# Two more quarter products by seven products, and x's two slots laid apart

## The chip, the cores and the metric

One core of a Trainium2 chip runs the whole kernel in one launch. The metric is the device time of that launch in microseconds (us), the median of several runs. A profile of one execution gives, for each instruction, its engine, its start and its length, all counted from the start of the profiled span. Five engines work side by side: TensorE (PE, matrix products; PEld is its loading of weights), VectorE (DVE), ScalarE (ACT), GpSimd (POOL) and SyncE (SP), which here only issues transfers. Transfers run on 16 DMA engines that all queues share.

## The reference

Four graph layers over the same 2048 x 2048 adjacency matrix `adj` and a batch `x` of 8 x 2048 nodes x 64 features, all fp32. Each layer adds its result to x and normalizes over the features.

```python
# layer 0: Chebyshev sum with weights that depend on the node
As = [eye, A, 2.0 * (A @ A) - eye]
w = einsum('nd,dkio->nkio', embedding, weight)      # d = 16
b = einsum('nd,do->no', embedding, bias)
x_g = einsum('knm,bmc->bnkc', stack(As), x)
x = layernorm(x + einsum('bnki,nkio->bno', x_g, w) + b)
# layer 1: twice relu((A @ z) @ W_i)
x = layernorm(x + z)
# layer 2: x @ w_self + (A @ x) @ w_neighbor + bias
x = layernorm(x + ...)
# layer 3: [x, Ax, 2AAx - x, Ax, 2AAx - x] @ weight + bias   (both supports are adj)
x = layernorm(x + ...)
```

So adj is applied to a 2048 x 512 matrix again and again. The first of these products, `A x` of layer 0, is the place of this change.

## The kernel before

**Layout.** The 2048 nodes are cut into 16 tiles of 128 (`NT`); the batch gives 512 columns (`BF`), handled as four pairs (`NP`) of two batch items x 64 features = 128 columns. `xy` holds x for every node tile and, in a second slot, another 512 columns per tile that serve as scratch and later as a second activation. In the kernel before, the two slots of a tile lie side by side in a partition: `[P, NT, 2, BF]`.

**Matrix products by seven.** A product of two 2 x 2 block matrices needs eight block products; with sums of blocks formed beforehand, seven do. The kernel uses this twice, one level inside the other. Seven big products stand for the whole of adj (`A11`, `A12`, `A22` and the sums `S1` to `S4`), and each of these may again be made of seven small ones with sums of its own quarter (`inner` in `prepare`, which writes four such sums; the function `inner` in `product` uses them). The sums of adj are formed once, in the first product, written to `comb` in DRAM, and read back by all later products (`load`, `product`).

**The first product, slice by slice.** adj comes in four slices of 512 output nodes (every slice takes one node tile out of each group of four), and each slice in four chunks `a` of 1 MB (`slice_chunk`), chunk j holding the inputs of node tiles 4j to 4j+3. `slices` are read into four ring buffers. While TensorE multiplies a slice, VectorE forms its sums (`prepare`, a generator that is advanced by `next(parts)` at chosen places), and GpSimd issues their stores to `comb`.

- Slice 0 (`plain_slice`) can't use sums of x yet, since x is still coming in. Chunks 2 and 3 (`AHEAD = (2, 3, 0, 1)`) are multiplied plainly for all four batch pairs, 32 matmuls of 512 columns into four PSUM banks (L868): for the first chunk node tile by node tile, for the second pair by pair. Chunks 0 and 1, that is the quarters (I, J) = (0, 0) and (1, 0) of adj, go through `two_level`: 28 matmuls of 128 columns (L828) that stand for 32, ScalarE copying each of the seven results out of PSUM (L832), and VectorE joining them (L843, L846) and adding the plain part (L887). Its sums of x, `t1`, lie in the scratch slot of `xy`.
- Slices 1 to 3 (`fast_slice`) use the seven big products with sums of x (`T`), matmuls of 256 columns (L914). One of them, with A22, goes through `two_level`.
- Between the products the pump (`pump.step`) puts small TensorE jobs: the biases (L735) and the turning back of each slice's result `hT` to node order (`back`, L461).

**What sets the order.** Instructions marked `keep_in_program_order` stay in the order of the program on their engine; the rest is placed by a scheduler. VectorE's sums are all marked. A transfer counts its completion on one of eight semaphores used in turn, for SyncE and ScalarE together, and waits until the transfer eight places before it is done. A buffer of a ring is written again when its last reader is through: `C` (four buffers, the `inner` sums), `T` (three, the big sums), `t` (five, the results `hT`), `a` (four, the chunks).

**The loads at the start.** SyncE issues the first chunk in four pieces of one node tile (L158), ScalarE x of the same four tiles in four pieces (L168: 128 columns of the first tile, its other 384, the second tile, the last two together). Then SyncE issues in turn x and a of the chunks 3, 0 and 1 (L171, L158). Before data is there, 11 matmuls on zeros keep TensorE busy (`rise`, L720).

Of the kernel before, what the change touches and what calls it, by code (L numbers as in the profile page):

```python
# [16 lines left out]
P = 128  # L17
EPS = 1e-5
GW = 512
# [85 lines left out]
def kernel(  # L105
# [42 lines left out]
    xy = big.tile([P, NT, 2, BF], F32, tag="xy", name="xy")  # L148
# [4 lines left out]
    def slice_chunk(ns, j, parts=1):  # L153

        a = ring.tile([P, TG, NG, P], F32, tag="a", name="a")
        for c in range(parts):
            m = ts(c, TG // parts)
            nc.sync.dma_start(a[:, m], slices[ns, j][:, m])  # L158
        return a
# [4 lines left out]
    chunks[0, AHEAD[0]] = slice_chunk(0, AHEAD[0], TG)  # L164

    for t, n, cols in ((0, 1, slice(0, 2 * F)), (0, 1, slice(2 * F, BF)), (1, 1, slice(0, BF)), (2, 2, slice(0, BF))):
        t += AHEAD[0] * TG
        nc.scalar.dma_start(xy[:, t : t + n, 0, cols], x[:, t : t + n, cols])  # L168
    for j in AHEAD[1:]:
        tq = slice(j * TG, (j + 1) * TG)  # L170
        nc.sync.dma_start(xy[:, tq, 0, :], x[:, tq, :])  # L171
        chunks[0, j] = slice_chunk(0, j)
# [12 lines left out]
    def xcol(slot, t, p):  # L185
        return xy[:, t, slot, ts(p, 2 * F)]

    def part(g, p, slot):
        return xy[:, g * TG : (g + 1) * TG, slot, ts(p, 2 * F)]
# [25 lines left out]
    def product(src, feature, between=None, rate=1, own=None, pin=False, runs=None, onto_slot=None, ends=False):  # L215
# [6 lines left out]
        def quarter(h, c):  # L222

            return xy[:, h * NT // 2 : (h + 1) * NT // 2, src, c * 4 * F : (c + 1) * 4 * F]
# [232 lines left out]
    def to_nodes(dst, pool, tiles, p, hT):  # L457
# [4 lines left out]
        nc.scalar.copy(xy[:, tiles, dst, ts(p, 2 * F)], pt)  # L462
# [4 lines left out]
    class Norm:  # L467
# [9 lines left out]
        def flat(self):  # L477
            return xy[:, self.tiles, self.slot, self.p0 * 2 * F : (self.p0 + self.n) * 2 * F]
# [59 lines left out]
        def store(self, t0=0, t1=TG):  # L538
            tiles = slice(self.tiles.start + t0, self.tiles.start + t1)
            for k in range(self.n):  # L540
                p = self.p0 + k
                nc.sync.dma_start(out[:, p, tiles], xy[:, tiles, self.slot, ts(p, 2 * F)])
# [38 lines left out]
    if True:  # L581
# [48 lines left out]
        def prepare(ns, ch, outers):  # L630
# [48 lines left out]

            outers[A22] = inner(A22, *raw(1, 1))  # L680
            yield
            inner(A12, *raw(0, 1))
            if ns == 0:

                sums_of_blocks()
                outers[A11] = inner(A11, *raw(0, 0))
                outers[A21] = inner(None, *raw(1, 0))
            outers[S1] = s1 = outer(rq(1, 0), rq(1, 1), ALU.add)
# [9 lines left out]
            if ns:  # L698
# [11 lines left out]
        with tc.tile_pool(name="p_n", bufs=4, space=PSUM) as p_n, tc.tile_pool(  # L710
# [30 lines left out]
            def xq(h, c):  # L741

                v = xy[:, h * NT // 2 : (h + 1) * NT // 2, 0, c * 4 * F : (c + 1) * 4 * F]
# [6 lines left out]
                xy[:, 3:NT:TG, 1, :].rearrange("p t (h c) -> p t h c", h=2),  # L750
                xy[:, 2:NT:TG, 1, :].rearrange("p t (h c) -> p t h c", h=2),
# [40 lines left out]
            def sums_t(b, t):  # L792
# [7 lines left out]
            b1 = [  # L800
                [by_tiles(xy[:, j * TG : (j + 1) * TG, 0, ts(2 * c + p, 2 * F)]) for j in range(2) for p in range(2)]
                for c in range(2)
            ]
            t1 = [[by_tiles(xy[:, c:NT:TG, 1, ts(n, 2 * F)]) for n in range(4)] for c in range(2)]
# [5 lines left out]
            def sums_of_blocks():  # L810
                for c in range(2):
                    sums_t(b1[c], t1[c])

            def two_level(raw, sums_, b, t, out):
# [11 lines left out]
                def mul(ps, n, x, start, to):  # L826
# [9 lines left out]
                mul(pa, 1, b21, False, out[:, 0, 0])  # L836
                mul(pb_, 6, t3, False, part[:, 2])
                mul(pa, 4, t1, True, out[:, 1, 1])
                mul(pb_, 3, t4, False, out[:, 0, 1])
                mul(pa, 7, b22, False, out[:, 1, 0])  # L840
                o = out.rearrange("p a b n -> p (a b) n")
                pin = tc.keep_in_program_order
                pin(nc.vector.tensor_tensor(  # L843
                    o[:, 1:], o[:, 1:], part[:, 0].unsqueeze(1).to_broadcast([P, 3, P]), ALU.add
                ))
                pin(nc.vector.tensor_tensor(o[:, 2:], o[:, 2:], part[:, 1:], ALU.add))  # L846
# [4 lines left out]
            def by_blocks(v):  # L851
                return v.rearrange("p (a b n) -> p a b n", a=2, b=2)
# [5 lines left out]
            def plain_slice(ns, ch, outers):  # L858


                ps = [bank() for p in range(NP)]
# [384 lines left out]
```

## Time and profile before

| | us |
|---|---|
| median of 3 runs | 1667.22 |
| all runs | 1666.92 to 1667.96 |
| profiled execution, its own time | 1667.24 |
| its span, first to last instruction | 1665.5 |

The first 200 us, and the end, in stretches: busy time of each engine and, in brackets, its instructions; then the granted clock of TensorE (1.00 is full), the share of time the DMA engines were busy, and what they moved.

| stretch, us | what runs | PE busy | DVE busy | PEclk | DMA share | GB/s |
|---|---|---|---|---|---|---|
| 0 to 6 | warming matmuls | 4.94 | 0.17 | 1.00 | 0.59 | 160 |
| 6 to 34 | slice 0, chunks 2 and 3 | 28.00 | 15.53 | 1.00 | 0.99 | 370 |
| 34 to 59 | slice 0, four quarters | 25.00 | 24.80 | 1.00 | 0.87 | 318 |
| 59 to 111 | slice 1 | 51.58 | 48.16 | 1.00 | 0.99 | 365 |
| 111 to 200 | slices 2 and 3 | 89.00 | 66.42 | 1.00 | 0.88 | 317 |
| 1640 to 1666 | the end | 18.39 | 18.03 | 0.92 | 0.25 | 73 |

How to read the profile: a line of the timeline gives the start, the busy time, the engine, the source line, the operation, the tile written and the tiles read, their shapes and the count; in brackets stands the idle time before it and what ended that. An fp32 matmul leaves two records, so x64 are 32 matmuls. Records of matmuls overlap, so the time of one is read from the distance between starts. L12 is line 12 of the kernel. In a row on a load, the last number is the time from its issue to its landing.

### The profile page before, as it was taken

Reading aid. Unit: us, or ns where it says so; the run is one execution under the profiler, and the core shown is the slowest. Engines: PE = TensorE matmul, PEld = TensorE weight load, DVE = VectorE, ACT = ScalarE, POOL = GpSimd, SP = SyncE. Lnnn points to the kernel's source line nnn. Section 1 sums busy time; section 2 is a strip of 40 time slices with the busy share of each in tenths; the row PEclk is TensorE's granted clock in tenths of the full one; section 3 lists DMA queues with packets and bytes.
Section 4 is the critical chain, followed back from the end, with each engine's and each line's share of the span. In section 5 each row is a group of like instructions: output and inputs, shape, how many; then the busy total and the mean of one; then the engine's idle time right before and its main releaser. Section 6 shows DMA issues by size and latency. Waiting matters only on the chain.

```text
span 1665.5 us, 21273 instructions
## 1 busy us (share of the span) xinstructions
PE 1656.5 (99%) x8414; PEld 1060.5 (64%) x8414; DVE 965.7 (58%) x1737; ACT 276.2 (17%) x811; POOL 245.6 (15%) x332
## 2 busy tenths in 40 slices
PE   9999999999999999999999999999999999999998
PEld 6988844444444444444454455599998455579998
DVE  5986895656456456655434365873668344453657
ACT  0200110242142144430010011220001011100001
POOL 1221200254155056550000000000000000000000
PEclk9999999999999999999999999999999999999999
DMA  8998899504503600029878877667888856678894
GB/s 316 339 385 310 319 319 326 201 26 163 204 26 128 250 26 26 26 67 363 291 262 279 303 256 258 231 213 275 292 295 300 304 210 237 227 263 297 311 317 162
DMA packets 82499, 391.57 MB, mean 235 GB/s; under 512 B 8960, under 2 KB 25600, under 8 KB 42848
## 3 DMA queue, kind: packets, MB, share of 16 engines
q1 hardware_dynamic: 69584, 346.78, 59.2%
q0 software_dynamic: 11248, 42.08, 6.7%
q10 hardware_dynamic: 1568, 1.35, 0.3%
q8 instruction: 67, 1.10, 0.3%
q14 instruction: 32, 0.26, 0.0%
HBM read 339.85 MB, written 50.33 MB: 234 GB/s over the span
## 4 chain that ended last, share of the span: by engine, by line
PE 99%; DVE 0%; ACT 0%; issue 0%; DVEq 0%; ACTq 0%
PE y L1089 20%; PE mmb L276 17%; PE mma L276 12%; PE mmc L276 12%; PE mmb L269 9%; PE ps_n L914 7%; PE mma L269 6%; PE mmc L269 6%; PE ps_i L828 3%; PE z L1141 3%; PE z L1170 2%; PE ps_n L868 2%; PE pt L1132 1%; PE pt_n L461 0%; PE rise L720 0%; PE mmd L269 0%
## 5 line engine op out<-in xcount | busy, mean ns | idle before, releaser
L276 PE MATMUL mmb<-a,t 128*128 128x512 f32 x648 | 292.0, 593 | 0.0
L1099 DVE SCALAR_TENSOR_TENSOR xy<-y,e_sb,xy 128x128 f32<-128x128 f32 x512 | 179.6, 351 | 141.2 <-PE y L1089 125.3
L276 PEld LDWEIGHTS mmb<-a,t 128*128 128x128 f32 x648 | 121.5, 190 | 145.3 <-issue 143.3
L1108 POOL TENSOR_TENSOR s<-s 128x512 f32<-128x512 f32 (+2 forms) x192 | 157.1, 818 | 333.4 <-ACT s L1103 323.2
L1103 ACT ACTIVATE s<-y,e_sb 128x128 f32<-128x128 f32 x512 | 139.2, 383 | 231.6 <-PE y L1089 231.6
L227 DVE TENSOR_TENSOR u<-mmb,p 128x512 f32<-128x512 f32 x84 | 57.9, 689 | 177.6 <-PE mmb L276 122.2
L269 PE MATMUL mmb<-t,a 128*128 128x128 f32 x1344 | 156.9, 275 | 0.0
L269 PEld LDWEIGHTS mmb<-t,a 128*128 128x128 f32 x1344 | 153.4, 192 | 0.0
L1089 PE MATMUL y<-wn,xT 64*128 64x512 f32 x512 | 131.5, 590 | 0.0
L1089 PE MATMUL y<-wn,C 64*128 64x512 f32 x512 | 131.2, 589 | 0.0
L1089 PE MATMUL y<-wn,tT 64*128 64x512 f32 x512 | 131.2, 589 | 0.0
L276 PE MATMUL mma<-a,T 128*128 128x512 f32 x256 | 115.5, 594 | 0.0
L276 PE MATMUL mmc<-a,t 128*128 128x512 f32 x216 | 97.3, 592 | 0.0
L291 ACT COPY p<-mma 128x512 f32<-128x512 f32 x42 | 24.7, 588 | 404.6 <-PE mma L276 247.3
L1089 PEld LDWEIGHTS y<-wn,xT 64*128 64x128 f32 x512 | 49.3, 187 | 61.2 <-issue 60.7
L1089 PEld LDWEIGHTS y<-wn,C 64*128 64x128 f32 x512 | 49.6, 187 | 60.2 <-issue 60.2
L1089 PEld LDWEIGHTS y<-wn,tT 64*128 64x128 f32 x512 | 49.6, 187 | 60.3 <-issue 60.3
L276 PE MATMUL mma<-a,xy 128*128 128x512 f32 x192 | 86.7, 593 | 0.0
L276 PEld LDWEIGHTS mma<-a,T 128*128 128x128 f32 x256 | 47.6, 190 | 56.8 <-issue 56.5
L227 DVE TENSOR_TENSOR C<-mmc,C 128x512 f32<-128x512 f32 x48 | 33.2, 692 | 85.9 <-PE mmc L276 75.1
L276 PEld LDWEIGHTS mmc<-a,t 128*128 128x128 f32 x216 | 40.0, 190 | 45.4 <-issue 45.2
L1141 PEld LDWEIGHTS z<-wd,C 128*128 128x128 f32 x384 | 50.2, 191 | 21.8 <-issue 20.8
(157 smaller groups left out, 2113.3 us busy)
## 6 DMA issues: line engine op xcount, KB each, us to landing
a<-comb SPq DMA_DIRECT2D x240, 1024.0 KB, 4.8
a<-in_blocks SPq DMA_DIRECT2D x54, 1024.0 KB, 4.8
comb<-si POOLq DMA_DIRECT2D x28, 1024.0 KB, 6.3
a<-in_slices SPq DMA_DIRECT2D x15, 1024.0 KB, 9.0
comb<-so POOLq DMA_DIRECT2D x15, 512.0 KB, 8.5
t1T<-hT SPq DMA_DIRECT2D x16, 256.0 KB, 3.9
xT<-in_xT SPq DMA_DIRECT2D x16, 256.0 KB, 3.3
tT<-t1T SPq DMA_DIRECT2D x16, 256.0 KB, 3.2
```

Source lines behind the costliest of these rows:

```text
L227: nc.vector.tensor_tensor(out, a, b, op)
L269: nc.tensor.matmul(to, a[:, k, m, :], xb[:, m, :], start=(start and opens and m == 0), stop=(m == TG - 1), skip_group_check=True,)
L276: nc.tensor.matmul(ps, xb[:, m, :], a[:, :, m, :], start=(start and m == 0), stop=(m == TG - 1), skip_group_check=True,)
L828: nc.tensor.matmul(ps, x[:, m // 2, m % 2], s[n](m), start=(start and m == 0), stop=(m == TG - 1), skip_group_check=True,)
L868: mm = nc.tensor.matmul(ps[p], xcol(0, TG * j + m, p), ch[j][:, m], start=(n == 0 and m == 0), stop=(n == 1 and m == TG - 1), skip_group_c ...
L914: nc.tensor.matmul(ps[:, ts(p, GW // 2)], b(k, p), a(k // TG, k % TG), start=(start and p == k == 0), stop=(k == NT // 2 - 1), skip_group_ ...
L1089: mm = nc.tensor.matmul(y[:, b, :], terms[n][half, ts(k, P)], wn[half, n, h * DH : (h + 1) * DH, :], start=(n == 0), stop=(n == 2),)
L1099: nc.vector.scalar_tensor_tensor(acc, y[:, :, ts(d, F)], e, acc, ALU.mult, ALU.add)
L1103: nc.scalar.activation(s[:, d], y[:, :, ts(d, F)], AF.Copy, scale=e)
L1108: nc.gpsimd.tensor_tensor(s[:, :n], s[:, :n], s[:, n : 2 * n], ALU.add)
L1141: nc.tensor.matmul(z[:, k, :], aT[:, ts(k, P)], wd[:, w, :], start=(n == 0), stop=(n == len(terms) - 1),)
L1170: nc.tensor.matmul(z[n][:, k], xT[half, ts(k, P)], w[half], start=True, stop=True)
```

## The change

Five things are done at once.

1. Slice 0: of the plain product of chunks 2 and 3, the part for the output half I = 1 and the batch pairs 2 and 3 (the quarter J = 1, c = 1) goes through `two_level`, with A22's sums and four new sums of x. The plain matmuls of pairs 2 and 3 then have 256 columns and share one PSUM bank. Their order is new: for both chunks, first pairs 0 and 1 node tile by node tile, then pairs 2 and 3.
2. Slice 1: the product of A11, sixteen plain matmuls of 256 columns, goes through `two_level` with the sums of x that slice 0 used. A11's sums are therefore formed ahead of A12's.
3. `two_level` becomes a generator that yields between its matmuls and its closing adds, and these are three (of 256, 256 and 128 columns) instead of two (384 and 256).
4. `xy` becomes `[P, 2, NT, BF]`: a slot's 16 tiles are contiguous in a partition. All accesses to it follow.
5. The first chunk is loaded in three pieces, of one, one and two node tiles.

```diff
-    xy = big.tile([P, NT, 2, BF], F32, tag="xy", name="xy")
+    xy = big.tile([P, 2, NT, BF], F32, tag="xy", name="xy")
...
-    chunks[0, AHEAD[0]] = slice_chunk(0, AHEAD[0], TG)
+    chunks[0, AHEAD[0]] = slice_chunk(0, AHEAD[0], (1, 1, 2))
...
-        nc.sync.dma_start(xy[:, tq, 0, :], x[:, tq, :])
+        nc.sync.dma_start(xy[:, 0, tq, :], x[:, tq, :])
...
+            if ns == 0:
+                sums_of_blocks((1, 1))
             outers[A22] = inner(A22, *raw(1, 1))
             yield
+            if ns == 1:
+                outers[A11] = inner(A11, *raw(0, 0))
             inner(A12, *raw(0, 1))
             if ns == 0:
-                sums_of_blocks()
+                sums_of_blocks((0, 0), (0, 1))
+                yield
+            if ns == 0:
                 outers[A11] = inner(A11, *raw(0, 0))
                 outers[A21] = inner(None, *raw(1, 0))
+                yield
...
-            if ns:
+            if ns >= 2:
                 inner(A11, *raw(0, 0))
...
-                mul(pa, 7, b22, False, out[:, 1, 0])
-                o = out.rearrange("p a b n -> p (a b) n")
-                pin = tc.keep_in_program_order
-                pin(nc.vector.tensor_tensor(
-                    o[:, 1:], o[:, 1:], part[:, 0].unsqueeze(1).to_broadcast([P, 3, P]), ALU.add
-                ))
-                pin(nc.vector.tensor_tensor(o[:, 2:], o[:, 2:], part[:, 1:], ALU.add))
+                mul(pa, 7, b22, False, out[1][:, 0])
+                yield
+                def add(a, b):
+                    tc.keep_in_program_order(nc.vector.tensor_tensor(a, a, b, ALU.add))
+                add(part[:, 1:], part[:, :1].to_broadcast([P, 2, P]))
+                add(out[1], part[:, 1:])
+                add(out[0][:, 1], part[:, 0])
+                yield
...
-                ps = [bank() for p in range(NP)]
+                ps = [bank() for p in range(3)]
                 for n, j in enumerate(AHEAD[:2]):
-                    steps = [(p, m) for p in range(NP) for m in range(TG)]
-                    if n == 0:
-                        steps = [(p, m) for m in range(TG) for p in range(NP)]
-                    for k, (p, m) in enumerate(steps):
+                    for p, m in [(p, m) for m in range(TG) for p in range(2)] + [(p, m) for p in (2, 3) for m in range(TG)]:
+                        to, cols = ps[p] if p < 2 else ps[2][:, ts(p - 2, GW // 2)], NG if p < 2 else NG // 2
                         mm = nc.tensor.matmul(
-                            ps[p],
+                            to,
                             xcol(0, TG * j + m, p),
-                            ch[j][:, m],
+                            ch[j][:, m, :cols],
...
                 hT = [new_h() for p in range(NP)]
+                join = quarter(1, 1, 1, [by_blocks(hT[2 + p][:, ts(1, GW // 2)]) for p in range(2)])
+                next(join)
+                yield hT
+                next(join)
+                yield hT
...
-                pa = mul(bank(), raw(0, 0), x_of(0, 0))
                 p1 = sums.tile([P, GW], F32, tag="p1", name="p1")
-                nc.scalar.copy(p1, pa)
+                if ns == 1:
+                    for _ in two_level(
+                        lambda i, j: lambda m: ch[j][:, m, i], outers[A11], b1[0, 0], t1[0, 0], by_pairs(p1)
+                    ):
+                        pass
+                else:
+                    pa = mul(bank(), raw(0, 0), x_of(0, 0))
+                    nc.scalar.copy(p1, pa)
...
                     first4 = plain_slice(ns, ch, outers)
                     next(first4)
+                    next(parts)
+                    next(first4)
+                    next(parts)
+                    next(first4)
                     sums_of_x(0)
```

In the program as built, the order of the instructions differs from before only in slices 0 and 1, on every engine; in slices 2 and 3 the closing adds of A22's product are three instead of two. SyncE issues the same transfers in the same order, but for the first chunk's three pieces.

## The prediction

> **What bounds the kernel now.** First the page's chain of waits, for the engine that ends last; then TensorE's own waits, for where it is not busy; then the timelines of the first 83 us, where the change lies.
>
> ```profile
> PE 1656.5 (99%) x8414; PEld 1060.5 (64%) x8414; DVE 965.7 (58%) x1737; ACT 276.2 (17%) x811; POOL 245.6 (15%) x332
> PE 99%; DVE 0%; ACT 0%; issue 0%; DVEq 0%; ACTq 0%
> ```
>
> ```profile
> PE rise L720 <- DVE zero L717: 1.1, 1, 1.1
> PE ps_i L828 <- ACT part L832: 0.4, 1, 0.4
> PE pt_n L461 <- ACT xy L462: 0.3, 1, 0.3
> ```
>
> TensorE is busy 1656.5 of 1665.5 us and waits 1.8 us in three places; most of the other 7 us lie behind its last product. So the time falls only by TensorE work taken out, and rises by any wait put in. The work around the change, TensorE and then VectorE (start, duration, what):
>
> ```profile
> 1.06 5.06 PE L720 MATMUL rise<-zero 128*128 128x128 f32 x22 [1.06 <-DVE zero L717]
> 5.92 27.95 PE L868 MATMUL ps_n<-a,xy 128*128 128x512 f32 x64
> 33.70 1.05 PE L828 MATMUL ps_i<-a,xy 128*128 128x128 f32 x8
> ...
> 58.71 3.62 PE L914 MATMUL ps_n<-a,xy 128*128 128x256 f32 x16
> ...
> 68.18 1.06 PE L828 MATMUL ps_i<-a,xy 128*128 128x128 f32 x8
> 69.66 1.13 PE L828 MATMUL ps_i<-si,t 128*128 128x128 f32 x8 [0.42 <-ACT part L832]
> ...
> 75.10 3.62 PE L914 MATMUL ps_n<-a,xy 128*128 128x256 f32 x16
> 78.55 0.60 PE L461 MATMUL pt_n<-ident,hT 128*128 128x128 f32 x4
> 78.99 3.62 PE L914 MATMUL ps_n<-a,xy 128*128 128x256 f32 x16
> 82.44 0.60 PE L461 MATMUL pt_n<-ident,hT 128*128 128x128 f32 x4
> ```
>
> ```profile
> 33.47 2.36 DVE L636 TENSOR_TENSOR so<-a 128x1024 f32<-128x1024 f32 x2
> ...
> 42.54 0.56 DVE L843 TENSOR_TENSOR u<-u,part 128x384 f32<-128x384 f32 x1
> 43.14 0.42 DVE L846 TENSOR_TENSOR u<-u,part 128x256 f32<-128x256 f32 x1
> 43.48 0.75 DVE L887 TENSOR_TENSOR hT<-ps_n,u 128x256 f32<-128x256 f32 x2
> ...
> 68.83 0.69 DVE L636 TENSOR_TENSOR si<-si,a 128x512 f32<-128x512 f32 x1
> ```
>
> Each fp32 matmul leaves two records. A 512-column one takes (33.70-5.92)/32 = 0.868 us, a 256-column one (78.55-75.10)/8 = 0.431, a 128-column one (58.71-33.70)/112 = 0.2233. VectorE has no gap between 24 and 107 us. The 0.42 us wait at 69.66 is booked to ScalarE, whose copy was done at 69.59; but the matmul reads A22's second sum, which VectorE ends at 68.83+0.69 = 69.52. That is the wait to watch: VectorE's list is full just where TensorE wants its output.
>
> **The work taken out.** Slice 0: sixteen 512-column matmuls become 256-column ones, -16 x (0.868-0.431) = -6.99 us, and 28 of 128 columns come in, +28 x 0.2233 = +6.25: -0.74. Slice 1: the raw A11 product (two stretches of 3.45, 6.90 us) becomes 28 such matmuls: -0.65. Together -1.39 us, 0.08% of the span.
>
> **The start.** New order: for the first chunk only two batch pairs run per node tile before the next is wanted. Before, four did. So tile 2 is wanted at 5.92 + 4 x 0.868 = 9.4 us, not at 5.92 + 8 x 0.868 = 12.9. Its x comes with ScalarE's fourth load, the 512 KB one (loads: size, us from issue to landing):
>
> ```profile
> xy<-in_x ACTq DMA_DIRECT2D x1, 512.0 KB, 8.4
> xy<-in_x SPq DMA_DIRECT2D x1, 1024.0 KB, 8.6
> ```
>
> It is issued at 2.2 and lands 8.4 later, at 10.6 (SyncE's wait for it ends at 10.60). Tile 1's x lands at 7.8 where 7.65 is wanted. Unchanged landings alone thus cost 1.2 us. Two edits move them. Three loads of a instead of four put the following 1 MB x load of the third chunk one place forward among the eight completion counters; it no longer waits for the first x piece (4.99 us) and goes out near 2.1, into the same 16 DMA engines. And x's rows become contiguous: 4 KB and 8 KB pieces instead of 2 KB. Whether that helps the 512 KB load depends on how two queues share. Here are the first loads of a and of x, both of 128 rows and issued at 0.75:
>
> ```profile
> a<-in_slices SPq DMA_DIRECT2D x1, 256.0 KB, 4.1
> xy<-in_x ACTq DMA_DIRECT2D x1, 64.0 KB, 4.2
> ```
>
> They land at 4.85 and 4.95: they shared by piece, not by byte. Counting pieces the 512 KB load (128 of 4 KB) would finish beside the 1 MB load (128 of 8 KB), after 3 MB in all. The trace's DMA rows have 2.2 MB moved by 9.1 us at 405 GB/s there, so 3 MB by 11.1, and with the 1 us that other loads need to report, 12.1: a wait of 2.7. Shared by byte it would land at 9.7: 0.3. I take 2.2, nearer the end that the pair of landings speaks for; ends 0.3 and 2.7.
>
> The Trainium skill, "DMA: Bandwidth & Descriptors", section "Queues, rings and completion order", speaks against this part of the change too: an engine takes turns between queue rows by whole packets, not bytes. By that rule alone the wait would be the 2.7 and the sum 0.5 higher; no run yet shows 8 KB pieces beside 4 KB ones.
>
> **VectorE.** Four subtractions for the new quarter (4 x 0.6 us) come before its first sum, in the idle time up to 16.35: hidden. Without that cover they would cost 2.4 us. The new quarter's three closing adds come after A21's sums, which end at 33.47, and before the outer sums. They wait for the quarter's last copy. TensorE ends the quarter at 33.70-0.74 = 33.0 plus the start's wait w, and a copy is out 0.47 after the product's slot (33.70 -> 35.06 less 0.89), so 33.5+w. From the rows at 42.54 to 43.48 I take 0.46+0.34+0.21 = 1.0 us for the three adds (bounds 0.7 and 1.6: the 256-wide op at its shortest pitch, and the 384-wide op three times less overlap), and 0.07 more for each of the four old quarters, 0.3. Queued behind them stand the outer sums, the S sums and A22's sums of slice 1, 69.52-33.47 = 36.05 us without a gap. A22's second sum is then out at 33.5+w+1.0+0.3+36.05 = 70.9+w. TensorE reaches slice 1's A22 product at 68.18-0.74+w = 67.4+w; in its new order ten of the 28 matmuls can go first (2.2 us), so it waits from 69.7+w to 71.0+w, 1.3 us. Before, the stretch 68.18 to 82.44 held 14.26-0.44 (a transpose) = 13.82 us for 13.15 of work: 0.67 of waiting. Added: +0.6; ends -0.67 (no wait left) and +1.5 (the adds at 1.6, and A12's sums finding their buffer 0.3 late).
>
> **What costs nothing.** A11's sums in slice 1 only move ahead of A12's: second sum at 70.9+w+1.2+2.53+1.33 = 76.0+w, wanted at about 75.9+w. If S4's sums ran over, that cover would be gone and each us be paid. Their buffer needs the S2 store, landed some 6 us after issue, 9 us before. A12's buffer is the S3 store, ended 69.5+w, issued 0.75 us long, landed 5.4 to 7.7 later, wanted at 77.2+w: just in time, the weakest cover. S1's first half is out at 80.9+w, wanted at 81.0+w. GpSimd's store of A11 goes out earlier; its queue has gaps of over 1.5 us there. Two transposes move behind S1 and S2; VectorE needs slice 0's buffer free only near 92. One slice-1 matmul is now ordered into the fourth quarter; its chunk (issued 39.30, 6.7 to land) comes some 0.6 late, and that is taken off the later 1.3 us wait. x of the last two chunks lands sooner than 24.06, but VectorE then only stands before the closing adds: 0. From slice 2 on VectorE has an idle 3.1 us (111.15), and the order on every engine is as before but for one more add under `A22`, so apart-slots cost or give nothing in the rest: VectorE's 2048-element ops take 2.29 us at either stride, by 46.46 (contiguous output) and 52.80 (strided). SyncE's queue holds the same transfers less one.
>
> **Sum** against the profiled execution's 1667.24 us (span 1665.5, and 1.7 around it; the median of the runs is 1667.22): -1.39 + 2.2 + 0.6 = +1.4, 1668.7 us. Ends -1.39+0.3-0.67 = -1.8 and -1.39+2.7+1.5 = +2.8: 1665.4 to 1670.1.
>
> **Rivals.**
> Only the sevens count: bytes are shared evenly, the first chunk comes in time and the wait at A22 stays as it was. For: 4 KB pieces, one load fewer. Against: the equal landings at 4.9. -1.39+0.3 = -1.1, 1666.1 us.
> The clock falls back: the start's wait is long enough for TensorE to lose the granted speed it has just risen to. The 11 warming matmuls took 5.06 us where 11 x 0.2233 = 2.46 would do: 2.6 us is the price of a cold start. 1668.7+2.6 = 1671.3 us, slower by 0.24%. It decides from an idle stretch long enough to be counted; in this trace only the last one shows a lower mean, 0.92 in the last 26 us with 7.6 idle. Against: the wait falls into two pieces of about 0.5 and 1.7.
> VectorE becomes the bound of slice 1: A12's buffer is not free because stores back up (7.7 us at 75 to 78). It decides once a store takes over 7; 1 to 2 us, then S1 late by as much: 1668.7+1.5 = 1670.2.
>
> **How the numbers follow.** Forecast 0.60, only the sevens 0.19, clock 0.13, VectorE 0.08. A measurement of this kernel tells some 0.2% (3.3 us) from no change: faster means under 1663.9, slower over 1670.6. Nothing found reaches 1663.9, since no more than 1.39 + 0.67 us is there to be won: 0.02 for what I overlook. Slower: the clock's 0.13 and half of VectorE's 0.08, 0.17. Same: 0.81. The range, 1665.4 to 1671.0, takes in the sevens and VectorE and ends just short of the clock.
>
> **What would show it.** In the new timeline: TensorE idle twice before 13 us, on x's loads, w in all (over 2 right, under 0.5 the sevens); 28 matmuls of 128 columns from about 29 us; the closing adds at 33.5+w; one wait near 71+w before A22's second sum, some 1.3; from 83 us on no new wait. A first chunk with longer records after the idle stretch speaks for the clock. An idle TensorE beyond slice 1, or a VectorE operation on x of another length, would prove the reasoning wrong.

## The result, and the profile after

| | before | after |
|---|---|---|
| median, us | 1667.15 (12 runs) | 1670.47 (12 runs) |
| all runs | 1666.92 to 1667.96 | 1670.18 to 1672.63 |
| profiled execution, its own time | 1667.24 | 1670.39 |
| its span | 1665.5 | 1668.6 |

The ratio is 1.0021, 95% interval 1.0013 to 1.0029: 3.3 us slower, just on the 0.2% that the prediction called the limit of what can be told. The forecast was 1668.7, its range 1665.4 to 1671.0.

The page of the changed kernel, busy time of the engines and the chain that ended last:

```profile
PE 1657.0 (99%) x8494; PEld 1067.2 (64%) x8494; DVE 971.0 (58%) x1754; ACT 279.5 (17%) x824; POOL 246.0 (15%) x332
...
PE 98%; DMA 1%; DVE 1%; ACT 0%; ACTq 0%; issue 0%; DVEq 0%; SPq 0%
```

TensorE's busy time is 0.5 us up although 1.4 us of work is gone: it is summed from records that overlap, and there are 80 more, of smaller matmuls. So the reading goes by starts. Transfers have come into the chain. Its waits (what waited, for whom, us in all, times, longest):

```profile
PE ps_n L893 <- DMA xy<-in_x: 2.1, 2, 1.2
PE rise L729 <- DVE zero L726: 1.1, 1, 1.1
PE ps_n L947 <- DMA a<-in_slices: 0.5, 1, 0.5
PE ps_i L841 <- ACT part L845: 0.4, 1, 0.4
PE ps_i L841 <- ACT u L845: 0.4, 1, 0.4
PE pt_n L462 <- ACT xy L463: 0.3, 1, 0.3
```

Before there was one such wait besides the first and the last of these; now there are five, in three places. TensorE's timeline shows the places:

```profile
5.92 2.38 PE L893 MATMUL ps_n<-a,xy 128*128 128x512 f32 x4
9.17 1.96 PE L893 MATMUL ps_n<-a,xy 128*128 128x512 f32 x4 [0.88 <-DMA xy<-in_x]
12.38 17.45 PE L893 MATMUL ps_n<-a,xy 128*128 128x512 f32 x56 [1.25 <-DMA xy<-in_x]
29.66 1.05 PE L841 MATMUL ps_i<-a,xy 128*128 128x128 f32 x8
...
50.01 0.70 PE L947 MATMUL ps_n<-a,xy 128*128 128x256 f32 x2 [0.54 <-DMA a<-in_slices]
...
71.20 1.06 PE L841 MATMUL ps_i<-a,xy 128*128 128x128 f32 x8
72.65 1.16 PE L841 MATMUL ps_i<-a,xy 128*128 128x128 f32 x8 [0.40 <-ACT part L845]
74.21 3.12 PE L841 MATMUL ps_i<-si,t 128*128 128x128 f32 x24 [0.40 <-ACT u L845]
...
79.20 1.16 PE L841 MATMUL ps_i<-a,xy 128*128 128x128 f32 x8
...
114.50 3.62 PE L947 MATMUL ps_n<-a,xy 128*128 128x256 f32 x16
```

Slice 2 begins at 114.50 (the last line), before at 110.95: +3.55. From there on the order is the old one, and the last product starts 3.55 later too (1658.21 against 1654.66). So the whole loss arises in the first 115 us. It divides so, each term read from starts:

| stretch | before | after | difference |
|---|---|---|---|
| slice 0's work | | | -0.74 |
| waits for x, 5.92 to 29.66: 23.74 us for 27.78 - 6.99 = 20.79 of work | 0 | 2.95 | +2.95 |
| wait for slice 1's chunk: 50.01, due at 49.31 (0.89 after the group before) | 0 | 0.70 | +0.70 |
| A22's product: 71.20 to 79.20, 8.00 us for 6.25 of work | 0.67 | 1.75 | +1.08 |
| A11's product to slice 2: 75.10 to 110.95, and 79.20 to 114.50 | 35.85 | 35.30 | -0.55 |
| sum | | | +3.44 |

0.1 us stays unexplained. The -0.74 is worked out from the price of one matmul. Four profiles without a wait at the start (e5_all, e9_pinned, e10_more, e12_plain_a11) bear it out: their plain phase takes 20.67 to 20.95 us where 20.79 was worked out. Behind the last product's start 10.39 us follow instead of 10.84, so that the execution is 3.15 longer and not 3.55.

The two waits for x, in the rows on the loads issued from 2.0 to 2.7 us (size, us from issue to landing):

```profile
xy<-in_x SPq DMA_DIRECT2D x1, 1024.0 KB, 9.9
a<-in_slices SPq DMA_DIRECT2D x1, 512.0 KB, 6.3
xy<-in_x ACTq DMA_DIRECT2D x1, 512.0 KB, 10.1
```

The 1 MB load of x now goes out at 2.14 (before 4.99), beside the 512 KB load, and the two land together, at 12.0 and 12.3; before, the 512 KB one came at 10.6. Tile 1's x (issued at 1.7, 7.4 us to land) comes at 9.1 instead of 7.8. For the sum of the two waits only the second landing counts: tile 2 was wanted at 9.4 and begins at 12.38, 2.98 later, however the wait is split.

VectorE, from slice 0's last copies to A22's second sum:

```profile
33.73 0.43 DVE L857 TENSOR_TENSOR part<-part 128x256 f32<-128x256 f32 x1 [0.90 <-ACT part L845]
36.41 0.63 DVE L857 TENSOR_TENSOR hT<-hT,part 128x256 f32<-128x256 f32 x2 [2.25 <-ACT hT L845]
36.95 2.36 DVE L637 TENSOR_TENSOR so<-a 128x1024 f32<-128x1024 f32 x2
...
46.04 0.42 DVE L857 TENSOR_TENSOR part<-part 128x256 f32<-128x256 f32 x1
46.56 0.63 DVE L857 TENSOR_TENSOR u<-u,part 128x256 f32<-128x256 f32 x2
47.30 0.76 DVE L921 TENSOR_TENSOR hT<-ps_n,u 128x256 f32<-128x256 f32 x2
...
73.44 0.69 DVE L637 TENSOR_TENSOR si<-si,a 128x512 f32<-128x512 f32 x1
```

VectorE stands still twice for the new quarter, and so starts its outer sums (36.95) 3.48 later than before (33.47). From there to A22's second sum it has no gap, but the stretch has grown: 36.95 to 74.13 is 37.18 us, before 36.05.

How A22's 1.75 us of waiting come about is seen in TensorE's order. Before, the seven products of `two_level` ran as written, one from raw quarters and one from sums in turn, each into the bank that the last but one had left; the only stop, 0.42, was 0.14 us behind VectorE's second sum. Now the scheduler has put the second raw product (72.65) right behind the first (71.20). Both use one bank, so it stands until ScalarE has copied the first out, 0.56 us by the starts (72.65 - 71.20 - 0.89), and the next again, 0.67 (74.21 - 72.65 - 0.89). VectorE's second sum is out just before that restart too, at 74.13; e3_defer, below, tells the two apart. The twenty matmuls behind take 4.99 us for 4.47 of work, 0.52. Sum 1.75.

### The profile page after: what moved, and what is told of

Same layout as the page of the kernel before. It is cut to its first block, busy times and chain, and to the rows that moved or that the text cites. A ratio compares the mean times of both kernels' runs of the same rounds, so it can differ in the third digit from the quotient of the medians.

```text
span 1668.6 us, 21480 instructions
## 1 busy us (share of the span) xinstructions
PE 1657.0 (99%) x8494; PEld 1067.2 (64%) x8494; DVE 971.0 (58%) x1754; ACT 279.5 (17%) x824; POOL 246.0 (15%) x332
## 3 DMA queue, kind: packets, MB, share of 16 engines
q10 hardware_dynamic: 1440, 1.35, 0.3%
## 4 chain that ended last, share of the span: by engine, by line
PE 98%; DMA 1%; DVE 1%; ACT 0%; ACTq 0%; issue 0%; DVEq 0%; SPq 0%
PE y L1133 20%; PE mmb L277 17%; PE mma L277 12%; PE mmc L277 12%; PE mmb L270 9%; PE ps_n L947 7%; PE mma L270 6%; PE mmc L270 6%; PE ps_i L841 3%; PE z L1185 3%; PE z L1214 2%; PE ps_n L893 1%; PE pt L1176 1%; DMA xy<-in_x 1%; DMA a<-in_slices 0%; PE pt_n L462 0%
```

## The experiments

The theory, as the expectations have it: a start that waits for x because the first chunk's order wants it earlier than its pieces come, and VectorE late at A22, eat what the sevens win. The rivals: the layout of the slots costs elsewhere; A11 by sevens loses by its sums what it saves; the clock falls back in the waits; at A22 it is ScalarE's copies. Each kernel was timed beside the kernel before on the same chip; "over before" is the difference of the medians.

| kernel | median, us | runs | over before, us | ratio, 95% |
|---|---|---|---|---|
| after | 1670.47 | 12 | +3.3 | 1.0013 to 1.0029 |
| e1_pieces | 1667.99 | 11 | +0.6 | 0.9996 to 1.0014 |
| e2_order | 1668.81 | 11 | +1.4 | 0.9999 to 1.0017 |
| e3_defer | 1669.04 | 11 | +1.7 | 1.0002 to 1.0020 |
| e4_inter | 1669.77 | 11 | +2.4 | 1.0006 to 1.0023 |
| e5_all | 1666.21 | 11 | -1.0 | 0.9986 to 1.0004 |
| e6_before_defer | 1666.25 | 11 | -0.9 | 0.9984 to 1.0001 |
| e7_loads | 1666.31 | 11 | -0.75 | 0.9985 to 1.0003 |
| e8_plain_a11 | 1671.78 | 10 | +4.6 | 1.0014 to 1.0033 |
| e9_pinned | 1666.36 | 11 | -0.8 | 0.9984 to 1.0002 |
| e10_more | 1665.87 | 11 | -1.2 | 0.9981 to 0.9998 |
| e11_filled | 1671.11 | 9 | +4.05 | 1.0014 to 1.0034 |
| e12_plain_a11 | 1666.86 | 11 | -0.2 | 0.9989 to 1.0007 |

The intervals reach some 1.5 us to each side. So a difference of half a us between two of these kernels rests on rows of their profiles, not on the medians.

### The start: pieces, order, layout

**e1_pieces**, the changed kernel with the first chunk in four pieces again:

```diff
-    chunks[0, AHEAD[0]] = slice_chunk(0, AHEAD[0], (1, 1, 2))
+    chunks[0, AHEAD[0]] = slice_chunk(0, AHEAD[0], (1, 1, 1, 1))
```

> The changed kernel with the first chunk in four pieces again, so that the third chunk's 1 MB x load waits for the first x piece (issue near 5.0 instead of 2.14). Theory (the loads crowd each other, counted by piece): x of tile 1 lands near 7.8 instead of 9.1, x of tiles 2 and 3 near 9.7 to 10.6 instead of 12.3; TensorE's start loss falls from 2.97 us to 0.3 to 1.4, and the time falls by as much, from 1670.5 to 1668.0 to 1668.9 us. Rival 1 (the x loads are as slow by themselves, at the rate of the DMA engines): landings and time stay, 1670 to 1671 us. Rival 2 (VectorE's list sets the end of slice 1, the start only moves the waiting): the start loss falls, but the wait at A22's sums grows by nearly as much, time not under 1669.8 us.

+0.6 instead of +3.3. Its profile is of an execution 1.5 us over its median, but the start can be read:

```profile
5.92 3.77 PE L893 MATMUL ps_n<-a,xy 128*128 128x512 f32 x8
10.40 17.45 PE L893 MATMUL ps_n<-a,xy 128*128 128x512 f32 x56 [0.72 <-DMA xy<-in_x]
27.68 1.05 PE L841 MATMUL ps_i<-a,xy 128*128 128x128 f32 x8
```

The four quarters begin at 27.68 instead of 29.66: of 2.95 us at the start 1.98 are the one load more or fewer. The second piece of x is back at 1.7 + 5.9 = 7.6, the 512 KB load at 2.2 + 8.1 = 10.3. What is left, 0.97, is the order's.

**e2_order**, the changed kernel with the first chunk multiplied tile by tile over all four pairs:

```diff
+                    steps = [(p, m) for m in range(TG) for p in range(2)] + [(p, m) for p in (2, 3) for m in range(TG)]
+                    if n == 0:
+                        steps = [(p, m) for m in range(TG) for p in range(NP)]
+                    for p, m in steps:
```

> The changed kernel with the first chunk's matmuls node tile by node tile over all four batch pairs. Tile 1 is then wanted at 8.5 and tile 2 at 11.1 or, after a wait for tile 1 (9.1), 11.8; landings unchanged at 9.1 and 12.3. Theory (the start loss is passed on whole): loss 1.2 us instead of 2.97, time 1668.7 us (1668.4 to 1669.2). Rival 2 (VectorE's list sets the end): time not under 1669.8 us.

+1.4. The loads are nearly the same (10.1 us for the 512 KB, tile 1's x at 9.4), but there is one wait, 1.44 us, for tile 1; tile 2 is then wanted late enough. The quarters begin at 27.97, 1.69 sooner. Its first product began at 5.05, 0.87 before that of the changed kernel's profiled execution, and stood the longer for tile 1.

**e4_inter**, the changed kernel with the two slots interleaved again, three pieces kept: `xy` is `[P, NT, 2, BF]`, and all accesses to it follow.

> The changed kernel with x's two slots interleaved by node tile again, all else as changed: x comes in 2 KB pieces, the first chunk in three loads. Theory (queues share by piece): x of tile 1 stays at 9.1, x of tiles 2 and 3 lands near 10.9 instead of 12.3, start loss near 1.6 instead of 2.97, time 1669.1 us (1668.7 to 1669.6). Rival (shared by byte, or smaller pieces just slower): x of tiles 2 and 3 no sooner than 12.0, time 1670.3 us or more. If the layout does anything to the rest of the kernel, a difference to the changed kernel that is not in the first 30 us would show it; theory and rival say none, under 0.3 us.

+2.4, 0.2 over what the theory allowed and under the rival's 1670.3. In the profiled execution tile 1's x lands at 8.3 and tiles 2 and 3's at 2.2 + 9.0 = 11.2 (apart: 9.1 and 12.3), and the quarters begin at 28.56. So 1.1 us of the start go to the layout: with the slots apart the 1 MB load has rows of 8 KB beside the other's 4 KB. The three shares found here, 1.98, 1.69 and 1.10, overlap: each is what one edit alone takes from the 2.95.

This run also answers the rival of a layout that costs elsewhere. From the quarters' start to slice 2 (113.01) it takes 84.45 us, the changed kernel 84.84, and the difference is the wait for slice 1's chunk (0.32 for 0.70). From slice 2 to the last product (1656.71) it takes 1543.70, the changed kernel and the kernel before 1543.71. So the layout costs and gives nothing behind the start.

**e7_loads**, the kernel before with the changed kernel's layout and pieces, its products untouched:

```diff
-    xy = big.tile([P, NT, 2, BF], F32, tag="xy", name="xy")
+    xy = big.tile([P, 2, NT, BF], F32, tag="xy", name="xy")
...
-    chunks[0, AHEAD[0]] = slice_chunk(0, AHEAD[0], TG)
+    chunks[0, AHEAD[0]] = slice_chunk(0, AHEAD[0], (1, 1, 2))
```

> The kernel before with the loads of the change alone: x's slots apart, the first chunk in three pieces (1, 1 and 2 tile pairs), the products as before. Theory: the pieces arrive as in the changed kernel (tile 1's x at 9.1 us, tiles 2 and 3 at 12.3), but the ten quarter products of each pair of tiles still take 7.0 us, so they are wanted at 5.92 + 3.5 = 9.4 and at 12.9: hidden, by 0.3 and 0.6; 1667.2, within 0.4. Rival, that the layout of the slots or the long row costs something in the rest: 1668 or more.

The landing times are the theory's (tile 1 at 9.5), and nothing is lost. But it is faster by 0.75 us, twice the 0.4 allowed: ten of the eleven runs lie at 1665.99 to 1666.63, under every one of the 31 runs of before (1666.78 and more). Its timelines, of TensorE and then VectorE:

```profile
5.21 3.75 PE L869 MATMUL ps_n<-a,xy 128*128 128x512 f32 x8
9.62 24.27 PE L869 MATMUL ps_n<-a,xy 128*128 128x512 f32 x56 [0.65 <-DMA xy<-in_x]
33.73 1.05 PE L829 MATMUL ps_i<-a,xy 128*128 128x128 f32 x8
```

```profile
23.68 4.43 DVE L797 TENSOR_TENSOR xy<-xy 128x512 f32<-128x512 f32 x7 [2.58 <-DMA xy<-in_x]
```

It starts 0.71 early and waits 0.65 for tile 1, so the quarters begin as before (33.70). Then two gains follow in this execution (1666.28, 0.96 under before's). VectorE's closed list begins with x's last chunks at 23.68, not 24.06; it is 0.4 early all the way to A22's second sum (69.12 for 69.52), and A22's product waits 0.24 instead of 0.67: slice 2 at 110.56, -0.39. And behind the last product 10.24 us follow, not 10.84. There SyncE's last wait, for the output's stores, is 0.7 instead of 1.2:

```profile
SPq L1239 <- PEq L1239: 1.0, 2, 0.8
SPq L1239 <- DMA out<-xy: 0.7, 1, 0.7
```

That end goes with the number of pieces: the seven profiled executions with four have 1.2 us there and 10.7 to 10.8 behind the last product, those with three 0.7 to 0.8 and 10.2 to 10.4, all but one (e8_plain_a11: 1.7 and 11.2). How one load at the start moves the last wait was not tried. Whether the layout brings x's last chunks sooner stays open: they are there at 23.0 to 25.1 in the eleven profiles with the slots apart, at 24.0 to 24.5 in the three with them interleaved.

### The wait at A22

**e3_defer**, the changed kernel with one 2.3 us sum of x taken from VectorE's list before A22's sums, and put in slice 1 behind A11:

```diff
+                if ns == 1:
+                    sums_of_x(2)
...
-                    sums_of_x(2)
```

> The changed kernel with one 2.3 us VectorE subtraction (the third sum of x, wanted only by S3's product after 104 us) moved from slice 0 to slice 1, behind the first results: A22's second sum is out near 71.8 instead of 74.1 us. Theory (VectorE's list, grown by the closing adds, is late at slice 1's A22 product and costs 1.1 us more than before): the wait inside that product, 1.75 us, goes to under 0.3, the time falls by 1.4 to 1.7 to 1668.8 to 1669.1 us. Rival (the start's 2.97 us is all of the loss and the waits at A22 are ScalarE's copies of the banks, not VectorE's sums): time stays, 1670.2 us or more.

+1.7: 1.6 us won. The profiled execution's waits:

```profile
PE ps_n L893 <- DMA xy<-in_x: 3.1, 2, 2.2
PE rise L729 <- DVE zero L726: 1.1, 1, 1.1
PE ps_n L947 <- DMA a<-in_slices: 0.5, 1, 0.5
PE pt_n L462 <- ACT xy L463: 0.3, 1, 0.3
```

Both lines on `ps_i` are gone, and A22's product takes 71.14 to 77.46, 6.32 us. But it doesn't show that VectorE was what TensorE waited for, as I expected: with the edit the scheduler also leaves the products in their written order, a raw one and one from sums in turn:

```profile
71.14 1.06 PE L841 MATMUL ps_i<-a,xy 128*128 128x128 f32 x8
72.04 1.12 PE L841 MATMUL ps_i<-si,t 128*128 128x128 f32 x8
```

The profiles with the other order speak against VectorE. In e1_pieces, second raw product and restart, then ScalarE's copy and VectorE's second sum before it:

```profile
71.44 1.16 PE L841 MATMUL ps_i<-a,xy 128*128 128x128 f32 x8 [0.40 <-ACT part L845]
73.00 3.12 PE L841 MATMUL ps_i<-si,t 128*128 128x128 f32 x24 [0.40 <-ACT u L845]
```

```profile
72.68 0.27 ACT L845 COPY u<-ps_i 128x128 f32<-128x128 f32 x1 [1.29 <-PE ps_i L841]
71.46 0.69 DVE L637 TENSOR_TENSOR si<-si,a 128x512 f32<-128x512 f32 x1
```

The second sum is out at 72.15, 0.85 before the restart; in the changed kernel it was 0.08 before it. The copy ends at 72.95, 0.05 before the restart, and so it does in the changed kernel (74.16). A22's product takes 8.00 us in both, and 8.0 in e2_order, e4_inter and e11_filled too; in e2_order and e4_inter TensorE even goes on before the second sum is out (72.08 for 72.44, 72.72 for 73.02). So in that order the 1.75 us are the copies' and the rival has it. VectorE's list acts through the scheduler: in the kernels with the new products that leave the order to it, a raw product is brought forward where the sum is not deferred (six) and not where it is (e3_defer, e5_all). How the scheduler decides is inferred from that. In the written order the changed kernel would, by its rows, have waited from 72.09 for the sum at 74.13: an estimate of 2.0 us, so the loss is the list's either way. That order alone was not tried in the changed kernel.

**e6_before_defer**, the same edit in the kernel before.

> The kernel before with only the third sum of x deferred from slice 0 to slice 1. Theory (VectorE was already late at slice 1's A22 product, 0.67 us of waiting inside it): the wait goes, time 1666.6 us (1666.4 to 1666.8), 0.5 to 0.7 under the kernel before. Rival (that wait is ScalarE's copy, as the profile books it): time as before, 1667.1 to 1667.4.

-0.9, a little more than expected; the interval just takes in 1, but ten of the eleven runs lie under all 32 of the kernel before. Here the order is the written one in both kernels:

```profile
67.93 1.06 PE L828 MATMUL ps_i<-a,xy 128*128 128x128 f32 x8
68.82 1.11 PE L828 MATMUL ps_i<-si,t 128*128 128x128 f32 x8
```

The 0.42 wait is gone: it was VectorE's. Slice 2 begins at 110.08, -0.87, of which 0.26 are a shorter plain phase (the quarters begin at 33.44).

### A11 by sevens

**e8_plain_a11**, the changed kernel with slice 1's A11 in eight quarter products, its sums back at their old place.

> The changed kernel with slice 1's A11 product plain again (its sums back at their old place), the new quarter of slice 0 kept. Theory (that product's saving is real and passed on: 6.90 us before, 6.35 in the changed profile): time up by 0.5 to 0.6 us to 1671.0. Rival (its saving is eaten by VectorE's later S sums, or by A12's buffer): time as changed or lower, 1670.5 us or less.

+4.6, 1.3 over the changed kernel instead of 0.5. It doesn't tell, since the profiled execution differs at the start: TensorE waits 2.68 us in one piece, and then the granted clock falls (the columns: us, busy time and instructions of PE, PEld, DVE, ACT, POOL, then the clock, DMA share, GB/s):

```profile
8.00:10.00 2.00, 0.00 (x0) 0.00 (x0) 0.00 (x0) 0.00 (x0) 0.00 (x0) 1.00 1.02 426
10.00:12.00 2.00, 1.91 (x4) 0.68 (x4) 0.00 (x0) 0.00 (x0) 0.00 (x0) 0.79 1.10 356
12.00:14.00 2.00, 1.94 (x3) 0.67 (x3) 1.13 (x2) 0.92 (x1) 0.00 (x0) 0.50 0.96 353
14.00:16.00 2.00, 2.00 (x6) 0.81 (x5) 1.54 (x4) 0.36 (x1) 0.00 (x0) 0.85 1.00 361
```

The 60 records behind the wait take 20.90 us (10.09 to 30.99), where 17.28 + 1.74 = 19.0 is what the changed kernel's rows give for them: 1.9 us for the clock. The edit also changes more than A11: the scheduler now puts matmuls of the plain product between the products of A22, and TensorE does not wait for the copies there.

**e12_plain_a11** asks the same of a kernel without that wait (e9_pinned, below).

> The pinned version of the three moves with slice 1's A11 product in eight quarter products instead of seven, so that only slice 0 keeps its new quarter. Theory: the sevens are worth 0.55 to 0.65 there as read from the profile, so slice 2 begins at 110.2 (109.64 with seven) and the time is 0.5 to 0.6 over the pinned version's: 1666.9. Rival, that what the sevens save in slice 1 is lost again in VectorE's sums: within 0.2 of the pinned version.

1666.86 against 1666.36: +0.5, the theory's figure, but the medians don't show it. The two kernels' runs overlap (1666.08 to 1667.84, 1665.50 to 1667.52), and five of the eleven executions here have 2.1 to 2.9 us outside their span, where the other six and all of e9_pinned have 1.7 to 1.9; by their spans both kernels have the median 1664.6. What shows the saving is the rows. From A11's start to slice 2 its profile has 110.57 - 74.71 = 35.86 us, e9_pinned's 109.64 - 74.44 = 35.20: 0.66. Slice 2's start lies 0.93 later; 0.5 of that is a first product that began 0.22 later and a plain phase 0.28 longer, and 0.22 less was waited in slice 0's quarters. A11 by sevens wins in its own stretch; that this reaches the end is not shown.

### Together

**e5_all**: the edits of e1_pieces, e2_order and e3_defer at once, both new sevens kept.

> The changed kernel with the three edits of the earlier runs together: first chunk in four pieces, its matmuls tile by tile over all pairs, the third sum of x deferred to slice 1. Theory (the 1.39 us of TensorE work are really saved, and the loss is the start's wait plus VectorE's lateness, both now gone): start loss under 0.4 us, wait inside slice 1's A22 product under 0.2, the wait for slice 1's first chunk (0.5 to 1.5 us, from one matmul that the order puts early) left; slice 2 starts 109.8 to 110.9 us against 110.95 before; time 1666.3 us (1665.9 to 1667.0). Rival (the seven products save nothing, since 28 small matmuls, seven copies and three adds cost as much as 32 columns' worth of plain ones): 1667.2 us or more.

-1.0, as expected. Neither x nor A22 is waited for, and the quarters begin at 26.80:

```profile
5.92 21.05 PE L896 MATMUL ps_n<-a,xy 128*128 128x512 f32 x64
26.80 1.05 PE L841 MATMUL ps_i<-a,xy 128*128 128x128 f32 x8
```

The runs fall into two groups, six at 1665.95 to 1666.21 and five at 1667.1 to 1667.33, and the profiled one is of the upper:

```profile
48.38 0.70 PE L950 MATMUL ps_n<-a,xy 128*128 128x256 f32 x2 [1.77 <-DMA a<-in_slices]
```

The one matmul of slice 1 that the scheduler put into slice 0's last quarter now waits 1.77 for its chunk.

**e9_pinned**: e5_all with the matmuls of `two_level` and of slice 1 kept in program order.

```diff
-                        nc.tensor.matmul(
+                        tc.keep_in_program_order(nc.tensor.matmul(
...
+                            if ns == 1:
+                                tc.keep_in_program_order(mm)
```

> As the run with the three edits, with the small matmuls of the quarter products and slice 1's first product pinned to program order, so that no matmul of slice 1 stands before the last quarter and waits there for its chunk. Theory: that wait (0.5 to 1.5 us) is paid in full once VectorE's lateness no longer covers it; without it the time falls by as much, to 1665.6 us (1665.2 to 1666.1), slice 2 starting near 109.5 us. Rival (covered by other waits): within 0.2 us of the run with the three edits.

A miss: no better in the median than e5_all. The chunk is no longer waited for, the two groups are gone and the fastest runs are faster (1665.5), but with TensorE early VectorE is late at A22 again: 0.55 us, and 0.37 in slice 0's last quarter.

**e10_more**: e9_pinned, and of the S quarters that slice 0 leaves to be summed, the second (S2) goes behind the third and behind slice 1's sums of A22 and A11 (the expectation calls it one of slice 1's).

> The pinned version of the three moves with VectorE's sums eased further: the second of slice 1's S quarters summed after A22's and A11's sums instead of before them. Theory: the wait of 0.55 us left at A22 goes, slice 2 begins at 109.0 to 109.2, and the time is 0.5 to 0.6 under the pinned version's: 1665.7. Rival, that the lateness moves on to the sums of A12 and of the S quarters, which go through the same buffers: within 0.2 of the pinned version.

-1.2 us, 0.5 under e9_pinned by the medians and 0.4 by the differences to before, and the one kernel here whose interval lies below 1. The wait at A22 is gone, but in the profiled execution slice 2 begins at 109.63, no sooner than e9_pinned's 109.64, since a wait of like length has come up before; TensorE, ScalarE and VectorE:

```profile
54.08 1.16 PE L843 MATMUL ps_i<-a,xy 128*128 128x128 f32 x8 [0.94 <-ACT part L847]
```

```profile
53.77 0.43 ACT L847 COPY part<-ps_i 128x128 f32<-128x128 f32 x2 [2.10 <-DVE u L859]
```

```profile
53.03 0.62 DVE L859 TENSOR_TENSOR u<-u,part 128x256 f32<-128x256 f32 x2
```

TensorE waits for a bank that ScalarE copies out, ScalarE for the `part` buffer that VectorE's closing adds of the third of the five quarters free at 53.65. This wait is not the edit's work. VectorE's list stood 0.57 later than in e9_pinned already at 43.53 (42.96 there), ahead of all that the edit moves: its sums behind x's last chunks began later (28.31 for 27.75), and TensorE was 0.18 earlier (26.19 for 26.37). So the median is the theory's, this profile neither shows the 0.55 as won nor speaks for the rival, and it does show that with TensorE ahead VectorE's list can be late in slice 0's quarters too.

What the two sevens bring is little all the same. The deferred sum alone, without them, has -0.9 (e6_before_defer); with them and all the rest it is -0.8 to -1.2. Of 1.39 us of work some 0.3 to 0.4 reaches the end by the best of these medians, less than they can tell apart; the waits at VectorE's list, 0.9 and 1.1 us in the last two profiles, take the rest.

### The scatter of the changed kernel

Eight of its twelve runs lie at 1670.18 to 1670.52, four at 1671.45 to 1672.63. **e11_filled** keeps TensorE busy in the start's waits:

```diff
-                        if n == p == m == 0:
+                        if n == 0 and p < 2 and m < 3:
                             tc.keep_in_program_order(mm)
+                        if n == 0 and p == 1 and m < 2:
+                            for k in range(6):
+                                tc.keep_in_program_order(
+                                    nc.tensor.matmul(rise[:, k % TG, :], zero, zero, start=True, stop=True)
+                                )
```

> The changed kernel with six 128-column matmuls of zeros (1.3 us) behind each of the first chunk's first two tile pairs, so that TensorE is not idle while x is awaited; they lie in time in which it waited (about 0.9 and 1.25 us). Theory, that the executions of the changed kernel that lie 1 to 2.2 us above the others are those in which the clock falls in these waits: none above 1670.8, median 1670.2 to 1670.6. Rival, that the scatter has another source: some executions at 1671.5 or more, as before.

A miss. Five runs at 1670.8 to 1671.11, four at 1671.63 to 1672.0: two groups 0.8 apart remain, with no idle stretch over 0.5 us at the start, and the lower one is 0.5 above the changed kernel's, since the zeros overran the second wait by some 0.4 (12.82 for 12.38). So the clock is not what parts these groups; e5_all has two groups, and its profile has no wait at the start. For the changed kernel's own upper runs the clock is not ruled out: its mean over the execution is 0.998 in two of the four (1671.52 and 1672.63) and 0.999 or 1.0 in the other ten runs, and 0.998 is also what the profiled execution of e8_plain_a11 has, whose start is the same and whose clock fell. A varying wait for slice 1's chunk (0.54 to 1.77 in the profiles with one) would fit, but no pair of profiles from both groups of one kernel shows it.

## Why the prediction was right, and where it was off

The forecast's case is what happened: less work, eaten by a start that waits twice for x and by a longer wait at A22. The median is 1.8 over the forecast, in the range. That it lies inside is in part luck. The two terms for the waits both came out over their upper ends (2.95 us at the start for 2.7, 1.78 behind it for 1.5), the sum's own upper end, 1670.1, was passed, and the median is inside because the range had been drawn wider for a rival. A tail 0.45 shorter, which was not foreseen, helped too. By the prediction's steps, from 1668.7 to the profiled 1670.39:

- **"The work taken out", -1.39.** Right: -0.74, as the plain phases without a wait bear out, and, for -0.65, -0.55 (0.66 between the rows of e12_plain_a11 and e9_pinned).
- **"I take 2.2, nearer the end that the pair of landings speaks for; ends 0.3 and 2.7".** Mis-sized by 0.75: 2.95, beyond the upper end. Sharing by piece gave nearly the landing (12.3 for 12.1): 0.5 of the 0.75 is the step down from 2.7 to 2.2, the rest the landing and the start behind it (12.38). Tile 1's x, left at 7.8, came at 9.1, which moved part of the wait forward and added nothing to it. That the 1 MB load goes out at 2.1 was right, and e1_pieces shows it to be 1.98 of the 2.95. The Trainium skill, "DMA: Bandwidth & Descriptors", section "Queues, rings and completion order", has an engine take turns between queues by packets, not bytes; the landings of the two loads, 12.0 and 12.3 though one has twice the bytes, agree with it if a packet grows with the row, and 11.2 in e4_inter, where both have rows of 2 KB, points the same way. The profile counts 1568 packets before and 1440 after on the queue of the 512 KB load, 128 fewer, as a packet for each row would have it.
- **"So it waits from 69.7+w to 71.0+w, 1.3 us. ... Added: +0.6".** This step failed, by 1.18: 0.70 at the chunk and 1.08 at A22, against 0.6. The chunk came as late as said, but was not taken off the later wait, since that wait hangs on the copies of a bank and follows TensorE wherever it is: A22's product takes 8.00 us in e1_pieces, which waited 1.46 for the chunk, and 8.01 in e4_inter, which waited 0.32. The prediction had ten matmuls go ahead for nothing; eight did, and paid 0.56 and 0.67 for their bank, and 0.52 behind. VectorE's second sum was foreseen well (70.9 + 2.95 = 73.85, measured 74.13), by two errors that nearly cancel: the outer sums began 0.5 sooner than said (36.95 for 33.5 + 2.95 + 1.0), and "0.07 more for each of the four old quarters" was some 0.27 (46.04 to 47.97 is 1.93, before 42.54 to 44.15 1.61; the others 1.86 for 1.60).
- **The tail**, taken as unchanged, is 0.45 shorter; it goes with the number of pieces, for a reason not found.

0.10 + 0.75 + 1.18 - 0.45 = 1.6 of the 1.7.

**The rivals.** "Only the sevens count", 1666.1, is not even reached by e5_all's 1666.21, which has the deferred sum besides. "The clock falls back", +2.6: not in the changed kernel's profiled execution (1.00 in all of its first 20 us), but in that of e8_plain_a11, at 1.9 us, and perhaps in two of the changed kernel's slowest runs. "VectorE becomes the bound", 1670.2: near in size, but not by its mechanism. VectorE has no gap from 36.95 to 113.7, so no store held one of its buffers; its list was simply full.

**"What costs nothing"** held from A11 on: no new wait behind 80 us. "Apart-slots cost or give nothing in the rest" held too: e4_inter differs from the changed kernel by 0.01 us from slice 2 to the last product.

## What to carry to other kernels

Taking work from an engine at 99% pays only as far as what feeds it can come sooner: find the engine whose list has no gap up to the point where the busy one wants its output, and ease that list first. Here moving one sum out of it won 0.9 us in the old kernel; with it, the new products, the first chunk in four pieces and multiplied tile by tile, a fixed order and one more sum moved, e10_more beats both kernels at 1665.87. The old products with the moved sum (-0.9 alone) and the three pieces (-0.75 alone) were not run together, so whether that time needs the new products at all stays open. And where a scheduler decides, a longer list on one engine can change the order on another: read the new order before pricing a wait by the old one.

## What the hardware showed

- A larger load beside a smaller one held it back to its own landing where its rows were longer: 512 KB at 12.3 beside 1 MB at 12.0 (rows of 4 and 8 KB), at 11.2 with rows of 2 KB for both, at 10.3 or 10.6 where the large one went out 2.7 or 2.85 us later. Each figure is of one execution; the five other profiles with rows of 4 and 8 KB beside each other have 12.2 to 12.7.
- The granted clock held through waits of 0.88 and 1.25 us and of 2.17 and 0.88 (e3_defer, 1.00 throughout), and fell to 0.50 after one of 2.68 (e8_plain_a11). The Trainium skill, "TensorE: Matmul & The Clock Gate", Part 1 on the clock gate, puts half rate behind an idle window of about 3.4 us; by the records the fall came after less (3.1 if the two matmuls before the wait took their usual 0.87 each).
- SyncE's last wait, at the end of some 1665 us, goes with the number of pieces of the very first load: 1.2 us in the seven profiled executions with four, 0.7 to 0.8 in six of the seven with three. What links the two was not found.
